# Predicting finished sequences by 64 ranks of both halves at once, with the features gathered eight turns ahead and one last scatter

## The chip, the cores, the metric

One core of one Trainium2 chip. The metric is the device time of one execution in microseconds (us). The kernel before took 2116.8 us (median of three runs, 2114.62 to 2117.16). All timed runs in this document that are compared are in the fast state; a single look is marked as one.

## The reference, cut to what matters

B = 1024 sequences of up to T = 100 steps, D = H = 128, all in float32. Each sequence has its own length from 1 to 100.

```python
_, gru_seq = scan(gru_step, h0, history)              # first recurrence
attn = softmax(where(mask == 1, mlp(feat, relu), -inf))   # attention over the steps
pooled = einsum('bt,btd->bd', attn, keys)             # keys = gru_seq
att_seq = pooled.T[:T]

def augru_step(h, inp):                               # second recurrence
    x_t, a_t = inp                                    # key of the step, its weight
    ti = concatenate([h, x_t])
    r = sigmoid(ti @ aug_Wr.T + aug_br)
    u = a_t * sigmoid(ti @ aug_Wu.T + aug_bu)
    h_hat = tanh(concatenate([h * r, x_t]) @ aug_Wh.T + aug_bh)
    return (1 - u) * h + u * h_hat

attention_feature = state of the second recurrence at step sequential_length - 1
comb = concatenate([user, item, hist_sum, item * hist_sum, attention_feature])   # 640
return mlp(comb, 640 -> 200 -> 80 -> 1, sigmoid)      # "the prediction" of one sequence
```

A sequence needs no more steps of the second recurrence after its last one, and its prediction can be made as soon as that step is done.

## The kernel before

The first part of the kernel (the first recurrence and the attention, up to about 1480 us) is not touched except for two index loads. In the second recurrence the sequences are sorted by length and dealt to two **halves** of up to 512. "Rank" 0 of a half is its longest sequence, so those that have ended are always at the upper end, and the width of the work shrinks from step to step, down to a least width of 96. One **turn** is one half's part of one step; the turns of the halves alternate. TensorE executes its products in order (the prediction shows one wait of 3.82 us that holds up every product behind it). The parts of the prediction's first layer that don't depend on the state are computed earlier and lie in DRAM as `part_d` (one row of 200 numbers a sequence); GpSimd gathers the rows of 128 ranks with an indirect DMA. The result is scattered to the sequences' places in `out`, again by GpSimd.

The prediction is a generator. Each `yield` ends a stage, and one stage is put in after each turn:

```python
def predict(g, i, pool, tag):             # ranks 128 g to 128 g + 127 of half i
    part = sp.tile([P, M0], F32, tag=f"part_{tag}", name="part3")
    gather(part, part_d, g, i)            # indirect DMA of GpSimd
    yield
    ...
    for j in range(n):                    # n = 2 chunks of MC = 100 features
        nc.tensor.matmul(p0[:, ts(j, P)], lhsT=part[:, ts(j, MC)], rhs=ident,
                         start=True, stop=False)
        nc.tensor.matmul(p0[:, ts(j, P)], lhsT=m0[:, 4, ts(j, MC)],
                         rhs=h3[i][:, ts(g, P)], start=False, stop=True)
    yield
    # ... sigmoid, yield; second layer, yield; sigmoid, yield; third layer, yield
    y = sp.tile([P, 1], F32, name="y")
    nc.scalar.activation(y, p2, AF.Sigmoid, bias=later["c2"])
    nc.gpsimd.indirect_dma_start(out=out..., out_offset=..., in_=y, in_offset=None)
```

The loop starts the predictions when the width falls to a multiple of 128 or below it (a **crossing**; here after steps 26, 51 and 76), and the first 128 ranks of each half are left for the end:

```python
for t in range(1, T):
    ...
    for i in range(NH):                   # NH = 2 halves: two turns a step
        half_step(t, i)
        for _ in range(due.pop(0) if due else 0):
            next(ahead, None)             # row gathers for the next window of keys
        if jobs:
            try:
                next(jobs[0])             # one stage of the oldest prediction
            except StopIteration:
                jobs.pop(0)
    left = widths[t + 1] if t + 1 < T else 0
    for g in range(1, GH):
        if left <= g * P < widths[t]:
            jobs += [predict(g, i, pa, "a") for i in range(NH)]
    if t == T - G:                        # G = 4
        final = [predict(0, i, ps, "g") for i in range(NH)]
        ...
# the end: last state, then the stages of both final predictions; each scatters to `out`
```

The row gathers matter later. The keys of the second recurrence are brought in by windows of 8 steps, and GpSimd gathers the rows of the next window while this one is worked on. `due` deals them to the turns:

```python
def spread(q):
    ahead = 2 if widths[FIRST[q]] > HB // 2 else 3        # steps left free at the end
    n = NH * -(-widths[FIRST[q]] // R)                    # row gathers of the window
    slots = NH * (FIRST[q] - (FIRST[q - 1] if q > 2 else 1) - ahead)
    done = [-(-j * n // slots) for j in range(slots + 1)]
    return [b - a for a, b in zip(done, done[1:])]
```

## Time and profile before

| | before |
|---|---|
| median of the first three runs | 2116.8 us |
| span of the profiled run | 2110.0 us |
| TensorE / VectorE / GpSimd / ScalarE busy | 97% / 83% / 62% / 39% |
| mean granted clock of TensorE (share of full speed) | 0.986 |
| second recurrence, from turn 2 to the start of the last sigmoid of the reset gate | 600.8 us |

A turn is read as the time from one start of the reset gate's sigmoid on ScalarE to the next (line 984 before the change, 991 after it). In this document and its expectations, turns are numbered by these starts, turn 2 being the one that starts at 1493.47 us here; turn n belongs to step (n + 2) / 2, rounded down. A step has two turns. In the profile's lines PE is TensorE, PEld its loading of weights, DVE VectorE, ACT ScalarE, POOL GpSimd and SP SyncE.

The prediction shows the stalled first prediction of a crossing. Here is the second one of the same crossing, some eight turns later, which found its features ready. The timeline of TensorE in the kernel before (start, length, line, what, output <- inputs, instructions in the group; the trace has two records for a float32 product, its two passes, hence x2; lengths overlap, so starts are compared):

```profile
1764.98 0.38 PE L1025 MATMUL p<-ident,part 128*100 128x128 f32 x2
1765.20 0.38 PE L1028 MATMUL p<-h,m 128*100 128x128 f32 x2
1765.42 0.38 PE L1025 MATMUL p<-ident,part 128*100 128x128 f32 x2
1765.64 0.38 PE L1028 MATMUL p<-h,m 128*100 128x128 f32 x2
1765.86 0.78 PE L964 MATMUL ph<-r,wh 128*128 128x364 f32 x2
```

From 1764.98 to 1765.86 the four products of the first layer take 0.88 us, 0.22 each, at full clock. That is what the first layer of a prediction costs TensorE when nothing is waited for (its later layers add 0.66 us to two more turns); all else at a crossing is loss.

And the end, which the prediction tells by its chain of waits, in the timeline of ScalarE and GpSimd (in brackets: idle before, and what ended it):

```profile
2099.35 1.00 POOL L1055 DMA_INDIRECT out<-y,idx  x1 [24.45 <-ACT y L1054]
2099.40 0.26 ACT L1054 ACTIVATE y<-p,c 128x1 f32<-128x1 f32 x1 [0.33 <-PE p L1051]
2103.08 0.98 POOL L1055 DMA_INDIRECT out<-y,idx  x1 [2.73 <-issue]
```

The second half's result `y` is there at 2099.66. GpSimd has by then issued the first scatter, and stands until 2103.08 before it issues the second.

### The profile page before, as it was taken

To read this page: it belongs to the slowest core of one execution; us is meant where nothing else is said; L and a number is where in the kernel's file an instruction comes from. 1 tells how busy PE (TensorE), PEld (TensorE's weight loads), DVE (VectorE), ACT (ScalarE), POOL (GpSimd) and SP (SyncE) were. 2 spreads that over 40 slices of the span, in tenths; PEclk is the share of its full clock that TensorE was granted. 3 is DMA by queue.
4 is the path that set the end of the run, shared out by engine and by line. 5 is a ranking of instruction groups with operands and counts; after the bars stand their busy time and mean duration, and the time that the engine had idled before them with its cause. 6 is when DMAs were issued, how large, how long until landed. Compare 5 with 4: busy or idle time off the path is not lost. (4 is left out here: it accounts for less than half of the span.)

```text
span 2110.0 us, 26649 instructions
## 1 busy us (share of the span) xinstructions
PE 2049.9 (97%) x8260; PEld 985.6 (47%) x8260; DVE 1760.0 (83%) x3025; ACT 826.8 (39%) x1508; POOL 1301.5 (62%) x1301
## 2 busy tenths in 40 slices
PE   8999999999999999999999999996999999999987
PEld 3343333333333333333333333333444556788987
DVE  6888999988989888989898888996567767886865
ACT  3334343433334343334333434332444434444544
POOL 0234939479887969595969494996633534444322
PEclk9999999999999999999999999998999999999998
DMA  4543233333323343333423333313533423333321
GB/s 118 113 92 101 87 101 109 109 95 96 97 88 93 112 121 110 94 109 109 141 88 100 101 101 88 92 45 91 165 93 93 116 85 89 98 106 82 79 60 32
DMA packets 253555, 205.59 MB, mean 97 GB/s; under 512 B 74790, under 2 KB 215818, under 8 KB 253402
## 3 DMA queue, kind: packets, MB, share of 16 engines
q1 hardware_dynamic: 241082, 171.36, 29.2%
q0 software_dynamic: 12320, 32.44, 5.5%
q8 instruction: 67, 1.10, 0.2%
q14 instruction: 86, 0.70, 0.1%
HBM read 147.68 MB, written 54.40 MB: 96 GB/s over the span
## 5 line engine op out<-in xcount | busy, mean ns | idle before, releaser
L483 PE MATMUL ps<-x,wih 128*128 128x512 f32 x1200 | 592.6, 603 | 4.1 <-DMA x<-in_hist_x 4.1
L483 PE MATMUL ps<-hn,whh 128*128 128x512 f32 x1188 | 574.7, 593 | 0.0
L483 PEld LDWEIGHTS ps<-x,wih 128*128 128x128 f32 x1200 | 221.2, 191 | 327.2 <-issue 257.8
L483 PEld LDWEIGHTS ps<-hn,whh 128*128 128x128 f32 x1188 | 226.0, 190 | 283.8 <-issue 275.2
L469 POOL TENSOR_TENSOR xm<-x,m 128x512 f32<-128x512 f32 x200 | 244.6, 1223 | 128.3 <-DMA m<-mask_d 128.0
L514 ACT ACTIVATE ps<-ps,bih 128x512 f32<-128x512 f32 x200 | 132.4, 662 | 473.5 <-DVE ps L513 473.5
L495 ACT ACTIVATE r<-ps,brz 128x512 f32<-128x512 f32 x200 | 137.4, 687 | 391.3 <-PE ps L483 390.2
L470 POOL TENSOR_TENSOR hist<-hist,xm 128x512 f32<-128x512 f32 x200 | 266.1, 1330 | 15.7
L573 POOL TENSOR_TENSOR pooled<-pooled,kw 128x512 f32<-128x512 f32 x190 | 255.8, 1346 | 14.9
L572 POOL TENSOR_TENSOR kw<-kt,e 128x512 f32<-128x512 f32 x190 | 220.3, 1159 | 64.1 <-DVE e L728 64.0
L157 POOL DMA_INDIRECT rows<-keys_d,idx_k x208 | 202.1, 972 | 83.1 <-POOL rows L156 50.0
L552 DVE TENSOR_TENSOR kq<-hn,item 128x512 f32<-128x512 f32 x200 | 228.2, 1180 | 0.0
L631 PE MATMUL pm<-hn,wk 128*32 128x512 f32 x1200 | 213.3, 598 | 5.6 <-DVE f L665 3.6
L631 PE MATMUL pm<-kq,wkq 128*32 128x512 f32 x1200 | 210.7, 594 | 0.0
L972 ACT ACTIVATE c<-ph,bh 128x96 f32<-128x96 f32 (+42 forms) x198 | 96.7, 488 | 277.8 <-PE ph L964 245.9
L631 PE MATMUL pm<-mv,w 128*32 128x512 f32 (+1 forms) x808 | 198.0, 601 | 2.4 <-ACT mv L670 1.9
L988 DVE TENSOR_TENSOR pu<-pu,c 128x96 f32<-128x96 f32 (+42 forms) x197 | 88.9, 451 | 120.4 <-ACT c L972 107.2
L156 POOL COPY rows<-rest 128x1 f32<-128x1 f32 x208 | 39.1, 188 | 232.2 <-DVE rest L998 225.6
L665 DVE TENSOR_TENSOR f<-pm,q 128x512 f32<-128x512 f32 x200 | 128.4, 683 | 54.5 <-PE pm L631 54.4
L518 DVE TENSOR_TENSOR d<-hn,ps 128x512 f32<-128x512 f32 x198 | 136.1, 687 | 34.9 <-ACT ps L514 32.6
L519 DVE TENSOR_TENSOR d<-ps,d 128x512 f32<-128x512 f32 x200 | 138.4, 692 | 23.9 <-ACT ps L515 7.4
L513 DVE TENSOR_TENSOR ps<-ps,u 128x512 f32<-128x512 f32 x200 | 140.0, 700 | 21.5 <-PE ps L483 0.5
(158 smaller groups left out, 3040.5 us busy)
## 6 DMA issues: line engine op xcount, KB each, us to landing
x<-in_hist_x SPq DMA_DIRECT2D x212, 256.0 KB
keys_d<-kt SPq DMA_DIRECT2D x46, 1024.0 KB
m<-mask_d SPq DMA_DIRECT2D x200, 128.0 KB
keys_d<-kt SPq DMA_DIRECT2D x64, 64.0 KB
rows<-keys_d,idx_k POOLq DMA_INDIRECT x208
s_b<-mv SPq DMA_DIRECT2D x200, 8.0 KB
mask_i<-in_mask SPq DMA_DIRECT2D x8, 200.0 KB
at<-att_d SPq DMA_DIRECT2D x32, 48.0 KB
```

The source lines that it names most:

```text
L157: nc.gpsimd.indirect_dma_start(out=r[:, k, :], out_offset=None, in_=keys_d[q], in_offset=bass.IndirectOffsetOnAxis(ap=idx_k[:, k, i : i + ...
L469: nc.gpsimd.tensor_mul(d, x, m)
L470: nc.gpsimd.tensor_add(acc, acc, d)
L483: nc.tensor.matmul(p, lhsT=w[:, g, :], rhs=v, start=(j == 0), stop=(j == len(parts) - 1),)
L495: nc.scalar.activation(r, pr, AF.Sigmoid, bias=brz[:, 0:1])
L513: nc.vector.tensor_add(pi, pi, u)
L518: nc.vector.tensor_sub(d, h, pi)
L519: nc.vector.tensor_mul(d, pz, d)
L552: nc.vector.tensor_mul(kq, h, item[:, self.cols])
L572: eng.tensor_mul(d, k, w)
L573: eng.tensor_add(acc, acc, d)
L631: nc.tensor.matmul(p[i][s, :], lhsT=w[:, s], rhs=v, start=start, stop=stop)
```

## The change

Its intent: predict by 64 ranks of both halves together, as soon as these ranks have ended (by the number of sequences alive, not by the width, which never falls below 96); issue the gather at the crossing, but put the first product in only after eight turns; and make the last 64 ranks of both halves one prediction with one scatter. That makes seven predictions in the loop (crossings after steps 14, 26, 39, 51, 64, 76 and 89) and one at the end.

```diff
+ALIVE = [[min(HB, 2 * -(-r // (2 * EIGHTH))) for r in room] for room in ROOM] + [[HB] * T]
+WIDTHS = [[max(LEAST, n) for n in alive] for alive in ALIVE]
+PR = P // NH
...
+    idx_p = const.tile([P, HB // PR], I32, name="idx_p")
...                                       # beside the other index loads, near 660 us
+            for i in range(NH):
+                nc.sync.dma_start(out=idx_p[ts(i, PR), :].unsqueeze(2), in_=inv_d...)
...
-        def predict(g, i, pool, tag):
+        def predict(g, last=False):
...
-            gather(part, part_d, g, i)
+            rows_of(part, part_d, None, True)             # 64 ranks of both halves
...
+            def of_part(j):
+                nc.tensor.matmul(p0[j], lhsT=part[:, ts(j, MC)], rhs=ident,
+                                 start=True, stop=False)
+            def of_state(j, i):
+                nc.tensor.matmul(p0[j][:, ts(i, PR)], lhsT=m0[:, 4, ts(j, MC)],
+                                 rhs=h3[i][:, ts(g, PR)], start=False, stop=i == NH - 1)
+            if last:                      # half 1's products alone come last
+                for j in range(n):
+                    of_part(j)
+                for i in range(NH):
+                    for j in range(n):
+                        of_state(j, i)
+                    yield
+            else:
+                for j in range(n):
+                    of_part(j)
+                    for i in range(NH):
+                        of_state(j, i)
+                yield
...
-                if jobs:
-                    try:
-                        next(jobs[0])
-                    except StopIteration:
-                        jobs.pop(0)
-            left = widths[t + 1] if t + 1 < T else 0
-            for g in range(1, GH):
-                if left <= g * P < widths[t]:
-                    jobs += [predict(g, i, pa, "a") for i in range(NH)]
+                for n, job in enumerate(list(jobs)):
+                    job[0] += 1
+                    if n == 0 and job[0] > 2 * G and next(job[1], job) is job:
+                        jobs.remove(job)
+            left = alive[t + 1] if t + 1 < T else 0
+            for g in range(1, HB // PR):
+                if left <= g * PR < alive[t]:
+                    jobs.append([0, predict(g)])
+                    if left:
+                        next(jobs[-1][1])                 # the gather, at once
...
-                final = [predict(0, i, ps, "g") for i in range(NH)]
+                final = predict(0, last=True)
```

More of the change, by code (lines that the diff above doesn't have):

```diff
@@ L65 @@
 ROOM = [[EIGHTH * (HB + n) - FALL * t for t in range(T)] for n in SPARE]
-WIDTHS = [
-    [max(LEAST, min(HB, 2 * -(-r // (2 * EIGHTH)))) for r in room] for room in ROOM
-] + [[HB] * T]
+ALIVE = [[min(HB, 2 * -(-r // (2 * EIGHTH))) for r in room] for room in ROOM] + [[HB] * T]
+WIDTHS = [[max(LEAST, n) for n in alive] for alive in ALIVE]
+PR = P // NH
 @with_exitstack
@@ L389, in load_later @@
             )
+            for i in range(NH):
+                nc.sync.dma_start(
+                    out=idx_p[ts(i, PR), :].unsqueeze(2),
+                    in_=inv_d.rearrange("(g r i) o -> i r g o", r=PR, i=NH)[i][:, :, 0:1],
+                )
             place_i = pre.tile([P, KH, NH, 2], I32, name="place_i")
@@ L872, in gru_phase, with augru_phase @@
                 nc.sync.dma_start(out=to[p], in_=att[half.i][p * R : (p + 1) * R])
-    def augru_phase(pools, widths):
+    def augru_phase(pools, widths, alive):
         wp = pools.enter_context(tc.tile_pool(name="wp3", bufs=3))
@@ L1013, in last_state, with rows_of @@
             nc.vector.tensor_sub(h, u, rest)
-        def predict(g, i, pool, tag):
+        def predict(g, last=False):
             m0, m1 = later["m0"], later["m1"]
+            n = M0 // MC
+            pool, tag = (ps, "g") if last else (pa, "a")
+            def rows_of(out_ap, in_ap, o, i):
+                nc.gpsimd.indirect_dma_start(
+                    out=out_ap,
+                    out_offset=o and bass.IndirectOffsetOnAxis(ap=idx_p[:, g : g + 1], axis=0),
+                    in_=in_ap,
+                    in_offset=i and bass.IndirectOffsetOnAxis(ap=idx_p[:, g : g + 1], axis=0),
+                )
@@ L1018, in predict @@
             part = sp.tile([P, M0], F32, tag=f"part_{tag}", name="part3")
-            gather(part, part_d, g, i)
+            rows_of(part, part_d, None, True)
             yield
-            n = M0 // MC
             f0 = sp.tile([MC, n, P], F32, name="f0")
-            p0 = pool.tile([P, HB], F32, tag=tag, name="p0")[:MC, : n * P]
-            for j in range(n):
+            p0 = [pool.tile([P, HB], F32, tag=tag, name="p0") for _ in range(n if last else 1)]
+            p0 = [p0[j if last else 0][:MC, ts(0 if last else j, P)] for j in range(n)]
@@ L1025, in predict @@
+            def of_part(j):
                 nc.tensor.matmul(
-                    p0[:, ts(j, P)], lhsT=part[:, ts(j, MC)], rhs=ident, start=True, stop=False
+                    p0[j], lhsT=part[:, ts(j, MC)], rhs=ident, start=True, stop=False
                 )
+            def of_state(j, i):
                 nc.tensor.matmul(
-                    p0[:, ts(j, P)],
+                    p0[j][:, ts(i, PR)],
                     lhsT=m0[:, 4, ts(j, MC)],
-                    rhs=h3[i][:, ts(g, P)],
+                    rhs=h3[i][:, ts(g, PR)],
@@ L1032, in predict @@
                     start=False,
-                    stop=True,
+                    stop=i == NH - 1,
                 )
-            yield
+            if last:
[11 more added lines that the diff above has]
+                yield
@@ L1036, in predict @@
             for j in range(n):
                 nc.scalar.activation(
-                    f0[:, j, :], p0[:, ts(j, P)], AF.Sigmoid, bias=later["c0"][:, j : j + 1]
+                    f0[:, j, :], p0[j], AF.Sigmoid, bias=later["c0"][:, j : j + 1]
                 )
@@ L1054, in predict @@
             nc.scalar.activation(y, p2, AF.Sigmoid, bias=later["c2"])
-            nc.gpsimd.indirect_dma_start(
-                out=out.rearrange("(b o) -> b o", o=1),
-                out_offset=bass.IndirectOffsetOnAxis(ap=idx[:, g, 2 * i : 2 * i + 1], axis=0),
-                in_=y,
-                in_offset=None,
-            )
+            rows_of(out.rearrange("(b o) -> b o", o=1), y, True, None)
         def gathers(q):
@@ L1086, in augru_phase @@
         ahead, due = gathers(2), spread(2)
-        jobs, final = [], []
+        jobs, final = [], None
         for t in range(1, T):
@@ L1095, in augru_phase, with augru @@
                     next(ahead, None)
-                if jobs:
-                    try:
-                        next(jobs[0])
-                    except StopIteration:
-                        jobs.pop(0)
-            left = widths[t + 1] if t + 1 < T else 0
-            for g in range(1, GH):
-                if left <= g * P < widths[t]:
-                    jobs += [predict(g, i, pa, "a") for i in range(NH)]
+                for n, job in enumerate(list(jobs)):
[8 more added lines that the diff above has]
+                        next(jobs[-1][1])
             if t == T - G:
-                final = [predict(0, i, ps, "g") for i in range(NH)]
-                for job in final:
-                    next(job)
+                final = predict(0, last=True)
+                next(final)
         open_state(T - 1, 1)
-        next(final[0])
+        next(final)
         last_state(1)
-        for job in jobs:
+        for _, job in jobs:
             all_of(job)
-        next(final[0])
-        next(final[1])
-        while final:
-            for job in list(final):
-                try:
-                    next(job)
-                except StopIteration:
-                    final.remove(job)
+        all_of(final)
     with ExitStack() as pools, tc.manual_schedule():
         gru_phase(pools)
-    def augru(widths):
+    def augru(n):
         with ExitStack() as pools, tc.manual_schedule():
-            augru_phase(pools, widths)
+            augru_phase(pools, WIDTHS[n], ALIVE[n])
     over = nc.values_load(over_d, min_val=0, max_val=len(SPARE))
     with tc.If(over < 1) as fits:
-        augru(WIDTHS[0])
+        augru(0)
     with fits.Else():
         with tc.If(over < 2) as fits:
-            augru(WIDTHS[1])
+            augru(1)
         with fits.Else():
-            augru(WIDTHS[2])
+            augru(2)
 def _laid_out(np, r):
```

## The prediction

> **What bounds the kernel now.** The page first: TensorE (PE) is busy 97% of the 2110.0 us span, VectorE 83%, ScalarE 39%, GpSimd (POOL) 62%. The change hardly touches the first 1480 us (GRU and attention), so I read only the second recurrence, about 1490 to 2110 us, where everything it edits lies. It runs two halves of 512 sequences in turn, one "turn" per half and step, narrower every step. The sigmoid of the reset gate (ScalarE, line 984) starts once per turn, so the distance between its starts is the length of a turn. It falls smoothly, 5.5 us at 512 columns, 3.87 at 384, 2.6 at 256, about 1.45 at 96, and PE leaves no gap: three products with the state and three with the key, 6 x 0.31 x 2 us at 370 columns. From about 128 columns downward a product costs 0.22 us whatever its width, and the turn stays near 1.4.
>
> That smooth fall is broken at three places, where the prediction of finished sequences is put between the turns. The waits of PE, 1490 to 2110 us (who, for whom, total us, times, longest):
>
> ```profile
> PE p L1025 <- DMA part<-part_d,idx: 13.8, 4, 4.9
> PE pr L960 <- DVE k L950: 1.7, 3, 1.2
> ```
>
> Nearly all that PE waits for is the gather of the features `part`; the weight load beside it has three such waits, 10.8 us (the same stalls seen by PE's other row, so the two are not added). The timeline around one, ACT, PE and POOL picked out (start, length, instruction, idle before):
>
> ```profile
> 1730.34 0.95 POOL L133 DMA_INDIRECT part<-part_d,idx  x1 [0.31 <-issue]
> ...
> 1734.32 0.72 PE L1025 MATMUL p<-ident,part 128*100 128x128 f32 x2 [3.82 <-DMA part<-part_d,idx]
> ...
> 1736.11 1.49 PE L964 MATMUL ph<-r,wh 128*128 128x384 f32 x2
> 1737.39 1.48 PE L964 MATMUL pr<-h,wr 128*128 128x380 f32 x2
> ...
> 1739.93 0.82 PE L960 MATMUL pr<-k,wr 128*128 128x380 f32 x2
> ```
>
> The gather is issued one turn before its product is due, and needs 4.0 us from issue to that product; PE executes in order, so both halves stand still for 3.8 us. Then the same product takes 1.48 us, not 0.8: PE comes back at half clock and keeps it for 5.6 us. The stretches show it (us, busy PE, PEld, DVE, ACT, POOL, then the granted clock, DMA share, GB/s):
>
> ```profile
> 1700.00:1728.00 28.00, 28.00 (x86) 16.20 (x86) 22.29 (x43) 12.30 (x23) 14.45 (x26) 1.00 0.35 107
> 1730.00:1741.00 11.00, 7.18 (x20) 4.53 (x19) 2.89 (x7) 1.92 (x5) 3.32 (x6) 0.69 0.22 63
> 1900.00:1910.00 10.00, 5.81 (x20) 4.74 (x19) 2.54 (x8) 1.63 (x5) 3.29 (x6) 0.69 0.26 66
> ```
>
> Last, the end. The chain of waits that ended last (start, us, what):
>
> ```profile
> 2099.35 1.00 DMA out<-y,idx
> 2100.35 2.51 issue
> 2102.86 0.04 POOLq L1131
> 2102.90 0.18 issue
> 2103.08 0.98 POOL out L1055
> ```
>
> The second half's result is there at 2099.66, but its scatter starts only at 2103.08: both scatters write `out`, so the second waits until the first has landed. After it come 5.9 us to the end of the span, which any last scatter has.
>
> **What the Trainium skill says.** "TensorE: Matmul & The Clock Gate", What's actually happening: after an idle window of about 3.4 us the array runs at half clock until about 3.4 us of sustained work. The trace agrees: idle of 3.82, 4.2 and 4.9 us are each followed by half-speed products, while one of 0.93 us at 2015 is not (clock 1.00 there). "DMA: Bandwidth & Descriptors", Anatomy of one DMA: a DMA issued by GpSimd has a fixed 2.0 us, mostly the receipt of the write. Here 2.7 to 4.0 us pass from the start of the gather to the first product, and 3.5 us from the first scatter's start to the release of the second. "TensorE: Matmul & The Clock Gate", LDWEIGHTS: loading costs by the columns of the weights, so short products are bound by their weights; here 0.22 us per product (two passes, 0.11 each) at 96 as at 128 columns agrees.
>
> **The change part by part.**
>
> 1. *Stalls in the loop removed.* Before, each of three crossings (steps 26, 51, 76) starts two predictions of 128 columns, one per half. Their excess over the turns around them: from 1727.98 to 1785.87, 13 turns last 57.9 us; neighbours of 3.87 before and 3.51 after mean 3.69, so 48.0 without predictions: 9.9 lost. From 1898.77 to 1940.58, 41.8 against 13 x 2.415 = 31.4: 10.4 lost. From 2012.23 to 2046.76, 34.5 against 15 x 1.555 = 23.3: 11.2 lost. Sum 31.5 us. One turn in each carries most of it: 10.93 (normally 3.85), 9.62 (2.57) and 8.71 (1.45), over 7 us each, which is the idle, the slow clock after it, and the products themselves.
>
> 2. *The same work, put in without a stall.* After, there are seven predictions in the loop (64 ranks of both halves at a time: steps 14, 26, 39, 51, 64, 76, 89), and the gather goes out at the crossing, its first product from the ninth turn on. Eight turns are 35 us at the first and 8 x 1.4 = 11 us at the last, against 4 us of latency: no wait. What is left is PE's time. The second prediction at 1764 happened to be free of a stall: its turns took 0.87 more (four products, 0.22 each), then 0.43 (the four passes of the next layer) and 0.23 (the last): 1.5 us. After, the first layer has two products with `part` and four with 64-column states, six in place of four; at 0.22 each, weight-bound, 1.3 us. So 1.3 + 0.43 + 0.23 = 1.95 us per prediction. In the narrow turns, where ScalarE is used for about 1.0 of 1.4 us, its two sigmoids of 0.31 get in the way as well: the second prediction at 2036 cost 0.28 + 0.50 + 0.34 = 1.1 after its stall, with 1.3 for the first layer 2.4 us. Sum: 5 x 1.95 + 2 x 2.4 = 14.5 us.
>
>    Balance in the loop: 31.5 - 14.5 = 17.0 us saved.
>
> 3. *The end.* One prediction of 128 columns in place of two. Only the two 64-column products with the second half's state remain after its last update (h ends 2096.41), and they go to two banks, so the first sigmoid can start near 2096.9, not 2097.40; both end near 2097.5 instead of 2098.02. The rest of the chain is as before: result about 0.5 us earlier. Its scatter waits for nothing: start near 2099.4, not 2103.08: 3.7 us saved. The two gathers of the end become one; it was never waited for (issued at 2074, used at 2095).
>
> 4. *Added loads.* Two index loads of 4-byte elements, in the GRU stretch near 660 us. SyncE issues eight such loads there at 0.5 to 1.5 us each, is done at 664.1 and is next needed at 669.05; two more fit. Cost 0.
>
> Sum: 17.0 + 3.7 = 20.7 us of 2116.8: about **2096 us**; I say 2095.5.
>
> **The rivals.**
>
> *The gather wait is only moved.* If POOL were late, the gather would still be waited for, or the rows of the keys would. POOL issues a row gather every 1.45 us where it is busy (1945 to 1951), and around 190 columns it must issue 14 in 10 turns of 2.0 us: full. Without stalls it has less time to catch up. Against it: `pace` lets it wait 225.6 us for VectorE in this stretch, there is no wait for a row anywhere, and there is one gather and one scatter per crossing, not two at once. At the end the last gather stands behind the scatter of rank group 1 (its result about step 96, near 2086.5); it would start near 2087.9 and land by 2092, used at 2095.1: 3 us to spare. If it went wrong: 2099 to 2103.
>
> *PE becomes fuller than I think.* The predictions move to places where PE has no slack, and each has six first-layer products, not four. If each prediction costs 3 us: 2102. If 64 columns are cheaper than 0.22 us: 2 us less.
>
> *The stall was the whole loss and hidden noise stays.* Short hiccups that I can't put down to a wait (ScalarE idle 2.3 us before 1950.66; 1.2 us at 2075, followed by 3 us of slower clock) may vanish, move or multiply with another instruction stream: 4 us either way.
>
> **Range and chances.** Excess of the three places 2 us, cost of seven predictions 3, hiccups 4, as independent errors: about 5.5 us, so 2088 to 2103 for 8 in 10. Faster by over 2% needs 2074.5, more than everything the predictions cost in all (31.5 + 4): 2%. Slower by 2% needs a new stall at every crossing: 1%.
>
> **What would show it.** No wait of PE for `part` in the loop; granted clock 1.00 at the old places, no turn more than about 1.5 us above its neighbours there; seven places with about 2 us excess each; a single scatter at the end with no wait, 0.3 us after its result; the final result about 0.5 us sooner after the last sigmoid. Wrong would be: PE idle before `part` or VectorE waiting for rows; more than 3 us excess at each of seven places; the final gather waited for; or a GRU stretch that ends later than 1480.

## The result

| | before | after |
|---|---|---|
| median of six runs | 2114.55 us (2110.34 to 2117.16) | 2097.47 us (2093.76 to 2102.90) |
| ratio of fast runs | | 0.9923 (95%: 0.9904 to 0.9942) |
| profiled span | 2110.0 us | 2094.8 us |
| mean granted clock | 0.986 | 0.994 |

A ratio is the mean time of one kernel's fast runs over that of the other's of the same rounds, so it isn't quite the ratio of the medians quoted. By the ratio the change is worth 16.3 us of 2114.55, by the medians 17.1, in the two profiles 15.2. That is a change within 2%.

Where the 15.2 us of the profiles lie:

| stretch | before | after | saved |
|---|---|---|---|
| up to the first sigmoid of the second recurrence | 1476.81 | 1476.76 | 0.05 |
| from there to turn 2 | 16.66 | 18.47 | -1.81 |
| turn 2 to the last sigmoid of the reset gate | 600.79 | 586.88 | 13.91 |
| from there to the start of the last scatter | 8.82 | 5.17 | 3.65 |
| from there to the end of the span | 6.92 | 7.52 | -0.60 |

The -1.81 is ScalarE standing in the first turns of the recurrence, in part for what the profile names only as issue or as remote. The three profiles of kernels built on the one before have 16.7 to 17.1 us in that stretch, the ten of the one after and of kernels built on it (those on chips of ordinary speed) 16.7 to 20.2. So it varies from run to run, and a part may belong to the change. GpSimd issues gathers without a pause in this stretch (in the kernel after up to 1489.35 us; the kernel before had a pause of 1.83 us before 1485.08), so it may be the same thing as the late starts below. No experiment was made for it, and it stays open.

**The waits for the features are gone.** The waits of TensorE in the kernel after, 1500 to 2088 us, the longest groups (who, for whom, total us, times, longest):

```profile
PE pu L967 <- issue: 2.3, 4, 1.0
PE pu L967 <- ACT c L979: 2.1, 2, 1.9
PE pr L967 <- DVE k L957: 1.4, 4, 0.7
```

No line has `part` in it, where the kernel before had 13.8 us in four waits. What is new is `ACT c`: TensorE waits for a tanh of ScalarE, twice. That will be the main question below. The windows of the kernel after around the old crossings (start:end, length, busy time of PE, PEld, DVE, ACT and POOL with their instructions, granted clock, DMA share, GB/s):

```profile
1733.00:1744.00 11.00, 11.00 (x36) 6.63 (x35) 8.82 (x18) 4.77 (x9) 6.87 (x12) 1.00 0.44 123
1900.00:1910.00 10.00, 9.10 (x41) 7.66 (x42) 8.35 (x24) 5.13 (x12) 0.83 (x1) 1.00 0.26 66
2020.00:2030.00 10.00, 9.95 (x85) 9.49 (x85) 7.48 (x34) 5.38 (x20) 4.03 (x7) 1.00 0.32 69
```

The clock is granted in full, and in the first two TensorE executes 36 and 41 groups of products where stalled stretches of the same lengths had 20. The turn that carried the stall fell from 10.93 to 3.85 us at the first crossing and from 9.62 to 4.52 at the second. At the third the turn fell from 8.71 to 2.72, with a part of a prediction in it.

**What a prediction costs now.** The timeline of TensorE in the kernel after:

```profile
1760.21 0.38 PE L1045 MATMUL p<-ident,part 128*100 128x128 f32 x2
1760.43 0.48 PE L1050 MATMUL p<-h,m 128*100 128x64 f32 x4
1760.75 0.41 PE L1045 MATMUL p<-ident,part 128*100 128x128 f32 x2
1761.01 0.48 PE L1050 MATMUL p<-h,m 128*100 128x64 f32 x4
1761.33 0.83 PE L971 MATMUL ph<-r,wh 128*128 128x364 f32 x2
```

The six products of the first layer take 1.12 us (1760.21 to 1761.33), and the state's two with 64 columns take 0.32 between them: 0.16 each, where 128 columns took 0.22. Over the turns of a prediction the excess over the neighbours is 1.17 + 0.44 + 0.23 = 1.84 us, and 1.8 to 2.0 in the narrow turns: 13.0 us for all seven.

**The end.** The timeline of the kernel after, from the last state's products:

```profile
2084.32 0.57 PE L1050 MATMUL p<-h,m 128*100 128x64 f32 x4 [0.33 <-DVE h L1020]
...
2086.74 0.26 ACT L1089 ACTIVATE y<-p,c 128x1 f32<-128x1 f32 x1 [0.47 <-PE p L1086]
2087.28 0.99 POOL L1030 DMA_INDIRECT out<-y,idx_p  x1 [10.51 <-ACT y L1089]
```

One result, one scatter, 0.28 us after the result's end (2087.00), and no scatter before it to wait for.

**ScalarE is late at new places.** The sum doesn't close yet: 31.5 us of stalls less 13.0 for the seven predictions is 18.5, and the loop saved 13.9. The missing 4.6 us are in single turns without any prediction of their own. One of them, the longest, in the timeline of the kernel after (turns 131 and 132):

```profile
1968.19 0.97 POOL L159 DMA_INDIRECT rows<-keys_d,idx_k  x1 [0.27 <-issue]
1969.27 0.57 PE L971 MATMUL ph<-r,wh 128*128 128x180 f32 x2 [0.49 <-DVE r L997]
...
1971.07 0.97 POOL L159 DMA_INDIRECT rows<-keys_d,idx_k  x1 [0.27 <-issue]
...
1972.82 0.41 ACT L979 ACTIVATE c<-ph,bh 128x180 f32<-128x180 f32 x1 [3.69 <-PE ph L967]
1973.29 0.41 PE L967 MATMUL pu<-k,wu 128*128 128x174 f32 x1 [1.91 <-ACT c L979]
```

The product for the tanh is modelled to end at 1969.84, and the tanh starts at 1972.82. (The profile infers the releaser in the brackets, and names an earlier product into the same accumulator.) ScalarE has stood for 3.69 us, nothing of its own is in its way, and GpSimd issues row gathers back to back, with 0.27 us between them. Against the kernel before, such **late starts** of ScalarE cost 1.8 us more at turns 103 to 105 (where the old stall had hidden whatever there was), 1.0 more at 118 to 121 (2.1 were there before too), 2.8 more at 131 and 132 (1.25 before), and 2.1 in all at 166, 176 and 179. The kernel before loses 3.9 at turns 181 to 187, in a dip of the clock at 2077.9 us that the one after hasn't. That makes 7.7 less 3.9, or 3.8 of the 4.6 us; the rest isn't placed.

### The profile page after: what moved, and what is told of

The parts are those of the page before. It is cut to its first block, busy times and chain, and to the rows that moved or that the text cites. A ratio compares the mean times of both kernels' runs of the same rounds, so it can differ in the third digit from the quotient of the medians.

```text
span 2094.8 us, 26717 instructions
## 1 busy us (share of the span) xinstructions
PE 2042.1 (97%) x8292; PEld 977.6 (47%) x8292; DVE 1758.4 (84%) x3025; ACT 826.1 (39%) x1508; POOL 1302.3 (62%) x1301
```

## The experiments

Each is an edit to the kernel after unless it says otherwise. Ratios are to the kernel before on the same chip; 0.0001 of it is 0.21 us. All results are correct.

| experiment | median us (runs) | ratio (95%) |
|---|---|---|
| the change, first time | 2097.47 (6) | 0.9923 (0.9904 to 0.9942) |
| e_after_again | 2097.04 (5) | 0.9919 (0.9906 to 0.9933) |
| e_lead0 | 2122.05 (20) | 1.0037 (1.0028 to 1.0046) |
| e_lead1 | 2105.75 (16) | 0.9958 (0.9948 to 0.9968) |
| e_early_only | 2093.18 (4) | 0.9906 (0.9880 to 0.9933) |
| e_two_scatters | 2100.67 (5) | 0.9932 (0.9910 to 0.9954) |
| e_warm | 2106.26 (17) | 0.9975 (0.9966 to 0.9984) |
| e_wide_merged | 2092.19 (4) | 0.9898 (0.9881 to 0.9915) |
| e_act_shift | 2097.95 (one look) | |
| e_pool_burst | 2104.00 (one look) | |
| e_spread2 | 2089.28 (4) | 0.9889 (0.9872 to 0.9905) |
| e_best2 | 2093.03 (4) | 0.9910 (0.9894 to 0.9927) |
| e_best3 | 2079.47 (4; before 2102.48 on that chip) | 0.9892 (0.9875 to 0.9908) |

### Is it the early gather, or the sharing of the halves? (e_lead0, e_lead1, e_early_only)

The theory: the early gather makes the gain in the loop. The rival: fewer and better-placed predictions make it. Three kernels separate them. e_lead0 has the whole change but no lead of turns:

```diff
-                    if n == 0 and job[0] > 2 * G and next(job[1], job) is job:
+                    if n == 0 and job[0] > 0 and next(job[1], job) is job:
```

> The changed kernel with one constant altered: a prediction's first product comes in the turn right after its gather, as in the kernel before, not from the ninth turn on. Theory (the gain in the loop is the gather wait and the slow clock after it): PE again waits for the gather of part at most of the seven crossings, 2 to 5 us each, with the granted clock falling below 1[...]; 7 us lost per real stall, so 20 to 45 us slower than the changed kernel, 2117 to 2142 us, ratio to the kernel before 1.00 to 1.013. Rival (the gain comes from sharing one prediction between both halves, of which there are still eight): stays at 2095 to 2100 us, ratio 0.992.

It is slower than the kernel before: 1.0037, some 25 us above the change. The waits of TensorE, and a window at one crossing:

```profile
PE p L1045 <- DMA part<-part_d,idx_p: 18.6, 5, 5.7
```

```profile
1966.00:1976.00 10.00, 6.14 (x25) 6.15 (x26) 1.99 (x6) 1.75 (x5) 3.19 (x5) 0.66 0.14 42
```

Five of the seven crossings stall, by 3.7 to 8.9 us of excess a turn, and the clock in the window is granted at 0.66. So sharing the halves without a lead is worth less than nothing: it makes seven crossings of three. The crossings after steps 14 and 39 didn't stall, so the cost is under what seven stalls would be.

e_lead1 is the same edit with `job[0] > 1`: one turn more than e_lead0.

> The changed kernel with the first product in the second turn after the gather, one full turn ahead (4.3 us at the first crossing, 1.4 at the last). Theory: waits only where a turn is shorter than the 4 us from the gather's start to its landing, at most 2.6 us each[...]: 0 to 10 us slower than the changed kernel, 2097 to 2107 us, ratio to before 0.992 to 0.997, no slow clock at a crossing. Rival (any wait costs about 7 us, whatever its length): 3 or 4 stalls of 7 us, 2118 to 2125 us, ratio about 1.002 to 1.005.

The time fell in the middle, as expected, 7 to 8 us above the change. But the reason given for it was wrong: the waits were to be 2.6 us at most and the clock to stay full. The timeline of GpSimd and TensorE at one crossing:

```profile
1959.90 0.97 POOL L159 DMA_INDIRECT rows<-keys_d,idx_k  x1 [3.09 <-issue]
1961.18 0.95 POOL L1030 DMA_INDIRECT part<-part_d,idx_p  x1 [0.30 <-issue]
1964.02 0.75 PE L1045 MATMUL p<-ident,part 128*100 128x128 f32 x2 [3.95 <-DMA part<-part_d,idx_p]
```

The product waits 3.95 us, and the window from 1960 to 1970 us has the clock at 0.66 again; two crossings lost over 7 us each. The gather itself takes 2.84 us from issue to product. It was issued late: in GpSimd's queue it stood behind a row gather that itself started only at 1959.90. A lead that is counted in turns of the program is a lead in time only if the issuing engine is up to date.

e_early_only is the other side: the kernel before, with its predictions of 128 columns of one half and its two last scatters, and only the gathers issued at the crossing and used from the ninth turn on.

```diff
-                if jobs:
-                    try: ...
+                for n, job in enumerate(list(jobs)):
+                    job[0] += 1
+                    if n == 0 and job[0] > 2 * G and next(job[1], job) is job:
+                        jobs.remove(job)
...
-                    jobs += [predict(g, i, pa, "a") for i in range(NH)]
+                    for i in range(NH):
+                        jobs.append([0, predict(g, i, pa, "a")])
+                        if left:
+                            next(jobs[-1][1])
```

> The kernel before with nothing changed but the gather issued at the crossing and its first product from the ninth turn on; predictions stay 128 columns of one half, six in the loop and two at the end with two scatters. Theory: no wait for part in the loop; 31.5 us of excess shrink to six times 1.53 us = 9.2, so about 22 us less, and the end stays: 2090 to 2096 us, ratio to before 0.988 to 0.992, that is as fast as the whole change or up to 3 us faster. Rival (sharing the halves or the single scatter is the main part): 2103 to 2112 us, ratio 0.995 to 0.999.

2093.18 us, 0.9906: as fast as the whole change, though it keeps the slow end. In the profiles, its loop takes 580.71 us, where the change has 586.88 and, in its second profile, 583.14; its end, from the last sigmoid to the last scatter, takes 8.74, where the change has 5.17. So the theory held. The early issue makes all of the loop's gain, and the sharing of the halves adds nothing to it; only the end gains from it. The longest waits of TensorE in e_early_only, 1490 to 2070 us, have no `part` either; the first of them:

```profile
PE pr L960 <- DVE k L950: 3.3, 6, 1.0
```

### Is the one last scatter worth what was said? (e_two_scatters)

```diff
+            for _ in range(2 if last else 1):
                 rows_of(out.rearrange("(b o) -> b o", o=1), y, True, None)
```

> The changed kernel with the last scatter issued twice, the same 128 results to the same places (the result stays right), so that the second waits for the landing of the first as in the kernel before. Theory: 3.4 to 3.9 us slower than the changed kernel, 2100 to 2102 us, ratio to before 0.993 to 0.995, and the last scatter starts 3.7 us after the first. Rival (the end is hidden behind something else, such as what follows the last scatter): within 1 us of the changed kernel.

The same result is scattered twice. The timeline of GpSimd at the end:

```profile
2087.83 1.00 POOL L1030 DMA_INDIRECT out<-y,idx_p  x1 [11.17 <-ACT y L1089]
2090.94 0.99 POOL L1030 DMA_INDIRECT out<-y,idx_p  x1 [2.12 <-DMA out<-y,idx_p]
```

The second starts 3.11 us after the first, and the profile names the first scatter's landing as what it waited for. Expected were 3.4 to 3.9. By the ratios it costs 2 to 3 us; the intervals overlap, so the size rests on the trace, and the time only agrees in direction.

### How much of a stall is the slow clock? (e_warm)

The kernel before, with 14 products that nobody uses put in ahead of the waited-for one at the three stalled predictions, into the same accumulator:

```diff
+            if (g, i) in ((3, 0), (2, 0), (1, 1)):
+                for _ in range(14):
+                    nc.tensor.matmul(p0[:, :P], lhsT=ident[:, :MC], rhs=ident,
+                                     start=True, stop=True)
```

> The kernel before with 14 idle products of 128 columns (identity by identity, into the bank that the real ones then overwrite) put ahead of the three predictions whose gather PE waited longest for (3.8, 4.2 and 4.9 us); the wait for the gather stays. Theory (part of each 7 us is PE's half clock[...]): PE works 3.1 us of the wait, the granted clock stays 1.00 there, and each place loses 2 to 3 us less: 5 to 9 us faster than the kernel before, ratio 0.996 to 0.998. Rival (the clock isn't set by the idle, or its loss is hidden behind other waits): no faster than before, or 1 to 3 us slower.

```profile
1733.00:1744.00 11.00, 10.63 (x42) 6.89 (x43) 6.33 (x13) 4.62 (x10) 3.81 (x7) 1.00 0.28 71
1900.00:1910.00 10.00, 9.12 (x49) 8.35 (x50) 5.96 (x16) 4.75 (x12) 0.46 (x1) 1.00 0.14 42
2028.00:2037.00 9.00, 9.00 (x65) 8.88 (x66) 5.25 (x23) 4.40 (x15) 2.13 (x4) 0.81 0.13 30
```

The first and the third of these windows in the kernel before (the prediction shows the second):

```profile
1733.00:1744.00 11.00, 9.68 (x27) 6.34 (x28) 3.82 (x8) 3.35 (x7) 2.31 (x4) 0.69 0.13 42
2028.00:2037.00 9.00, 4.10 (x23) 3.92 (x22) 1.69 (x9) 1.06 (x4) 3.13 (x4) 0.81 0.23 55
```

With the added products the clock is full at the first two places (0.69 in the kernel before); at the third a dip stays (0.81 in both), after a wait of 1.86 us that the products did not fill. TensorE works through the wait, but the recurrence is still held up by it: the stalled turns take 8.59, 7.83 and 7.44 us where the kernel before had 10.93, 9.62 and 8.71. The kernel gains 5 us (0.9975), where the early gather alone gains 20 (0.9906). So the slow clock after the wait is a real part of a stall, 2.3 and 1.8 us of the stalled turn at the two places where the clock stayed full, and the wait is the larger part.

### Are 64 ranks a good size? (e_wide_merged)

The change with the products of 128 columns of one half back for ranks 128 and up (six predictions), ranks 64 to 127 of both halves as one, and the end as in the change:

```diff
+            if left <= PR < alive[t]:
+                jobs.append([0, predict(1)])              # ranks 64 to 127 of both
+                ...
+            for g in range(1, GH):
+                if left <= g * P < alive[t]:
+                    for i in range(NH):
+                        jobs.append([0, predict(g, i)])   # 128 ranks of one half
+                        ...
```

> A version meant to beat both: early gathers and the single last scatter of the changed kernel, but the ranks from 128 up predicted as 128 columns of one half (six predictions of 1.53 us), the ranks 64 to 127 of both halves as one (1.9 us), the ranks 0 to 63 of both at the end. Theory (products with the state are bound by their weights, so two 64-column products cost twice one of 128): the loop's predictions cost 6 x 1.53 + 1.9 = 11.1 us, not 7 x 1.88 = 13.2: 2 us faster than the changed kernel on the same chip. Rival (ScalarE's late starts, which move with the instruction stream, decide): anywhere between 4 us slower and 6 us faster.

0.9898 against 0.9919 for the change on the same chip: 4.4 us faster, expected 2. The intervals overlap (up to 0.9915 and down from 0.9906), so this is likely rather than shown. It does agree with e_early_only: the size of 64 ranks isn't where the gain is. (The "twice" of its theory doesn't hold: two products of 64 state columns took 0.32 us, one of 128 took 0.22.)

### What makes ScalarE late? (e_after_again, e_act_shift, e_pool_burst, e_spread2)

e_after_again is the change unaltered, on another chip, as a control.

> The changed kernel as it is, on the chip of the runs beside it, as their measure. Expected as it was timed: 2094 to 2102 us, ratio to before 0.990 to 0.994. Late starts of ScalarE, with its operands ready, near the turns 103, 119 to 121, 131 and 132, as in its first profile, if they belong to places in the program; elsewhere if they are chance.

The late starts are there again at turns 103 (1.98 us), 119 (2.25) and 131 and 132 (0.74 and 1.26). So they belong to places in the program, not to chance, though their sizes vary. The first theory was that they come at places of ScalarE's own instruction stream. e_act_shift moves that stream by 60 instructions:

```diff
                 half_step(t, i)
+                if 2 <= t <= 4:
+                    for _ in range(10):
+                        nc.scalar.copy(later["junk"], later["bh"])
```

> The changed kernel with 60 tiny ScalarE copies more in the steps 2 to 4, where a turn has 5.5 us and ScalarE works 2.6 of it, so that they cost little (under 3 us). It moves everything later in ScalarE's instruction stream by 60 instructions, which is about 12 turns. Theory (ScalarE's late starts belong to places in its own instruction stream): the starts late by about 2 us at the turns 103, 119 and 132 go to other turns, some 12 turns earlier. Rival (they belong to a time or to the DMA traffic of these steps): they stay at 103, 119 and 132.

They stayed: turns 103 (1.98), 119 (2.5), 131 and 132 (1.2 and 2.7). That theory fell. The next one was that GpSimd's row gathers, issued without a pause, delay ScalarE. e_pool_burst makes such a stretch where there was none, with ten more gathers after step 45 into a tile that nobody reads:

```diff
+            if t == 45:
+                for k in range(10):
+                    nc.gpsimd.indirect_dma_start(
+                        out=later["extra"][:, k, :], out_offset=None, in_=keys_d[WHOLE],
+                        in_offset=bass.IndirectOffsetOnAxis(ap=idx_k[:, 0, 0:1], axis=0))
```

> The changed kernel with ten row gathers more (into a tile that nobody reads), issued by GpSimd back to back after step 45, where it has nothing else to issue and where in no run ScalarE started late (turns of 2.9 us, about the turns 90 to 95). Theory (ScalarE and VectorE get the signals of TensorE late while GpSimd issues one indirect DMA after another without a pause): turns about 90 to 95 get longer by 1 to 5 us in sum, with tanh starting late by 0.6 us or more there, as at the turns 103, 119 and 132. Rival (GpSimd's queue has nothing to do with it): those turns stay at 2.91 to 2.79 us.

The timeline of ScalarE while they are issued:

```profile
1868.31 0.47 ACT L992 ACTIVATE pu<-pu,bu 128x282 f32<-128x282 f32 x1 [1.76 <-PE ph L971]
1876.06 0.50 ACT L979 ACTIVATE c<-ph,bh 128x282 f32<-128x282 f32 x1 [7.28 <-remote]
```

The standing, 7.28 us, begins within the burst: GpSimd's extra gathers follow one another by 1.25 us (two start at 1870.91 and 1872.16, the latter the last), and a scatter follows at 1873.41. The tanh starts 1.65 us after GpSimd is done with that. Turn 92 takes 10.68 us in place of 2.85, and turns 91 to 94 lose 10.4 us between them, where 1 to 5 were expected. TensorE stood for 5.1 us of it and came back at half clock, which is part of the loss. The direction is shown, by one look, at a place that had no late start; the size was mis-judged.

e_spread2 goes the other way and thins the gathers out: the same number is dealt to 12 turns, not 10, in the narrow windows.

```diff
-            ahead = 2 if widths[FIRST[q]] > HB // 2 else 3
+            ahead = 2
```

> The changed kernel with the row gathers of the narrow stages spread over 12 turns, not 10 (they end two steps before use, not three), which leaves GpSimd a pause between them: 16 gathers of 1.44 us in 31 us, not 26. Theory (the late starts of ScalarE at the turns 103, 118 to 121 and 131 to 132 come from GpSimd's unbroken row of gathers): their sum falls from about 8 us to under 4, and the time with it, 3 to 6 us under the changed kernel: ratio to before 0.989 to 0.991. Rival (the late starts belong to those places, not to the gathers): within 1 us of the changed kernel, 0.992, or slower if rows now come too late.

The timeline of ScalarE and GpSimd around turns 131 and 132:

```profile
1967.28 0.18 POOL L158 COPY rows<-rest 128x1 f32<-128x1 f32 x1 [0.66 <-issue]
...
1967.52 0.41 ACT L979 ACTIVATE c<-ph,bh 128x180 f32<-128x180 f32 x1 [1.15 <-PE pu L971]
...
1969.24 0.41 ACT L979 ACTIVATE c<-ph,bh 128x180 f32<-128x180 f32 x1 [0.74 <-PE ph L971]
```

GpSimd pauses between gathers, and the tanh stands for 0.7 to 1.2 us. At turn 103 the late start is gone, at 119 it is 0.74, at 131 and 132 it is 0.77 and 0.62: about 2 us in all, where the change had about 8. The kernel is at 0.9889, 6 to 7 us below the change by the ratios (its interval, up to 0.9905, overlaps that of the change's first runs, from 0.9904, and just misses that of its second, from 0.9906). So the theory held both ways: unbroken runs of row gathers make ScalarE late, and spreading them takes most of it away.

What stays open is how. The trace records the semaphore signals of the products before the late tanh up to 3 us after the modelled end of the product. Since ends of products are modelled, it can't be told whether the product, its signal or ScalarE's reading of it was late. (Around the late tanh of turn 132 four of these signals are recorded between 1972.80 and 1972.94 us, while the modelled ends of products are about 0.3 us apart. That looks like signals held back and passed on together, but proves nothing.) Nor do these edits part the issuing of gathers from their transfers, which come together. The share of DMA time alone doesn't decide it: it was 0.54 from 1968.00 to 1973.20 in the change, with the longest late start, but also 0.55 from 1962.00 to 1968.00 in e_spread2 and 0.54 from 1860.00 to 1868.00 in the first part of the burst, before the long standing.

### Does it add up? (e_best2, e_best3)

e_best2 is e_wide_merged with `ahead = 2`.

> The wide and merged version with the same spread over 12 turns. Theory: the two gains add: 5 to 8 us under the changed kernel, ratio to before 0.987 to 0.989. Rival: no better than the wide and merged version alone, 0.990.

It missed: 0.9910, no better than e_wide_merged alone. The trace has a new late start of 3.5 us at turn 104, where the gathers of the features of both halves are issued at once, and 1.2 us at 131. e_best3 issues the second half's gather four turns after the first's:

```diff
+                    if job[0] == 5 and job[2]:
+                        next(job[1])
```

> The wide and merged version with the row gathers spread over 12 turns, and the two feature gathers of a crossing no longer issued together: the second half's follows four turns later. Theory (in the version with both at once, ScalarE's late start of 3.5 us at turn 104 came from the two gathers joining a busy queue): that late start goes, and the 2 us that the wide predictions save come out: ratio to before 0.986 to 0.989, as fast as the spread version or up to 4 us faster. Rival (late starts move with any change of the instruction stream): ratio 0.990 or above, late starts of 2 us or more at other turns.

No late start over 0.55 us is left in the recurrence, yet the ratio, 0.9892, is the same as that of e_spread2 within its interval. (Its 2079.47 us are from a faster chip, where the kernel before took 2102.48; only the ratio may be compared.) The simplest better version is thus the change with one constant altered, e_spread2: by the ratios it is 6 to 7 us below the change (with intervals that barely part), and it beats the kernel before by 23.5 us in the same rounds' medians.

## Why the prediction was right, and where it was off

The time was right: 2095.5 us predicted, 2097.47 measured, inside 2088 to 2103 and within 2% of the kernel before, as forecast. The gain was not quite as right: 20.7 us predicted by the sum, 16.3 by the ratio, 15.2 in the profiles; the loop alone was to save 17.0 and saved 13.9. That the time was so close is in part luck: the kernel before ran at 2114.55 us in its six runs, 2.3 below the 2116.8 that the prediction started from, which hid about half of the difference.

1. **Stalls removed: right.** No wait for `part` is left, the clock is full at the old places, and without the lead the stalls come back (e_lead0). The early gather alone gives the loop's whole gain (e_early_only). What the prediction called the parts of a stall, "the idle, the slow clock after it, and the products themselves", was shown by e_warm, which took the slow clock away at two of the three places, left the wait, and got 5 us. One reading needs a limit: idles of 3.82, 4.2 and 4.9 us were followed by half clock and one of 0.93 was not, but the length of one idle doesn't settle it. In the kernel before 1.17 us of idle from 2075.88 came ahead of 3.41 us of half clock, and so did 1.86 us in e_warm, while 2.88 us from 1728.79 and 2.79 us from 2018.75 in e_lead0 left the clock full.

2. **The cost of seven predictions: a term was mis-sized, in the safe direction.** "At 0.22 each, weight-bound" took the 0.22 us of the old first-layer products for the time of their weights. Those products have weights of 100 columns and 128 moving columns (the columns that stream past the weights), and it was the moving columns that set the 0.22: with the same weights, a product of 64 state columns took 0.16 us, six products 1.12, not 1.3. The narrow turns cost 1.8 to 2.0, not 2.4. The sum was 13.0 us, not 14.5.

3. **The end: right.** The result was 0.51 us sooner (0.5 predicted), the scatter started 3.65 us sooner in all (3.7 predicted), 0.28 us after its result (0.3). The "5.9 us to the end of the span, which any last scatter has" (from that scatter's end) were 6.5, which takes 0.6 back.

4. **Added loads: right.** The two loads were issued at 658.6 and 659.3 us, and the first part ended 0.05 us sooner than before.

5. **The rival that came true was the third.** "Short hiccups that I can't put down to a wait" were put into the range as an error of either sign. They went against the change, by 4.6 us net in the loop, and one of the signs set out failed by it. "No turn more than about 1.5 us above its neighbours" at the old places: turn 103, at the second crossing, took 4.52 us, about 2 above the 2.57 of its neighbours. The hiccups weren't noise either. e_after_again has them at the same turns, and e_pool_burst and e_spread2 tie them to GpSimd's row gathers. The change left those gathers as they were, while the turns that they are dealt to became shorter. That the removed stalls had given GpSimd the pauses it now lacks is an argument from this, not shown by a run, and it isn't all: at turns 131 and 132, the longest late start, the change also has a feature gather in GpSimd's queue (at 1963.89), for its new crossing after step 64. e_early_only and e_wide_merged, equally free of stalls, have no crossing there, and their GpSimd has pauses; these turns take 1.74 and 2.17 us in both, where the change has 2.94 and 4.68. The prediction had seen that GpSimd is "full" there, but looked only for a wait for its data.

6. **The first rival, a gather that is only waited for elsewhere, did not come.** But e_lead1 shows how near it was in kind. With a lead of one turn more, GpSimd's backlog used up the lead. Eight turns are ample, as the prediction had worked out from 35 and 11 us against 4.

The second rival, a TensorE fuller than thought, fell with point 2.

## What to carry to other kernels

When a gather stalls an engine that executes in order, count what follows the wait too (here a clock at half speed for 3.4 to 6.8 us), and issue it earlier by a margin of *time* in which the issuing engine's own backlog has a place; merging work to have fewer gathers is a second matter and here gained nothing in the loop. Once a stall is gone, look at what the other engines do back to back in the shorter turns: here late starts during long runs of row gathers came to about 8 us, half as much as the whole gain, and dealing the gathers to two more turns took most of that back. And take the duration of a small product from a row with the same weights and the same width, not from one that is nearly alike.

## What the Trainium skill lacked or had wrong

- **Indirect gathers back to back delay another engine.** None of the skill's pages that I read for this case has it. The nearest, "DMA: Bandwidth & Descriptors", Issuing engines are not separate DMA queues, says that DMAs of all engines share the same 16 DMA engines and interleave; it speaks of transfers, while here ScalarE's compute starts late: before a tanh it stood for 3.69 us during a run of row gathers in the change and for 7.28 us with ten more of them, and for 0.7 to 1.2 us when they were spread (the DMA share was 0.54 at the first of these, and 0.55 with the gathers spread). How it comes about stays open.
- **A small product by both of its sizes.** "TensorE: Matmul & The Clock Gate", LDWEIGHTS, gives the load's time as the weights' columns over 1.2 in ns; from this one estimates 83 ns for 100 columns and 107 for 128. The trace agrees: 0.08 us a pass with 64 state columns and weights of 100 columns, 0.11 with 96 columns and weights of 128. What the section does not say, and what the prediction got wrong, is which of the two sizes binds a float32 pass: with weights of 100 columns, 128 moving columns took 0.11 us again. The larger of the two sizes fits all three.
- **The clock's return can take two windows.** The same page, What's actually happening, has about 3.4 us of sustained work to come back to full clock. In the kernel before the records show half clock for 6.83 us from 1733.14 and from 1903.81, about a microsecond before the wait's end, and for 3.41 us from 2033.51: once or twice the page's window, so an estimate by the page's single figure can be half of the loss.
- **The fixed time of a DMA issued by GpSimd is only a part of what a consumer waits.** "DMA: Bandwidth & Descriptors", Anatomy of one DMA — SWDGE (gpsimd) path, has a fixed 2.0 us. Here 2.8 to 4.0 us pass from the gather's start to the first product that uses it, and 3.11 us (e_two_scatters) to 3.7 us (the kernel before) from one scatter's start to the start of the next on the same tensor.
